# Layer 1's first product as seven block products, in a four-layer graph network on one Trainium2 core

## Chip, cores and metric

The kernel runs on one core of one Trainium2 chip. The metric is device time in microseconds (us) of one execution of the whole program: 2461.91 us is the median of 7 runs (2461.26 to 2463.57). All data are 32-bit floats, in the matrix products too. The engines are named as the profile names them: PE (TensorE, matrix products), PEld (its weight loads), DVE (VectorE), ACT (ScalarE), POOL (GpSimd), SP (SyncE, which issues most transfers).

## What is computed

128 graphs of 64 nodes with 256 features pass through four layers, each with a residual and a layer norm around it. Layer 0 is a gated graph network of five steps; layer 1, which the change touches, multiplies by a 256 x 1024 matrix, norms, and multiplies back; layer 2 is a hyperbolic aggregation; layer 3 an attention. Cut to what matters:

```python
# layer 0, five times (l = 0..4)
m = einsum('bnd,de->bne', h, weight[l])
agg = einsum('bij,bid->bjd', A, m)
h = gru_cell(agg, h, w_ih, w_hh, b_ih, b_hh)

# layer 1
neighbor_sum = einsum('bnm,bmd->bnd', adjacency, x)
agg = epsilon * x + neighbor_sum
h = einsum('bnd,dh->bnh', agg, W1) + b1          # 256 -> 1024, "the first product"
h = silu(h * rsqrt(mean(h*h, axis=-1) + 1e-6) * rms_weight)
out = einsum('bnh,hd->bnd', h, W2) + b2          # 1024 -> 256
```

The inputs hold `b1` = 0, `rms_weight` = 1 and `epsilon` = 0, but the kernel computes with whatever it is given.

## The kernel before, in words

**Tiling.** The graphs are taken in 16 groups of 8. Two graphs make one block of 128 rows, so a group is `NB` = 4 blocks, `R` = 512 rows. Most of a group's data is held with features on the 128 partitions: an array (128, `KD` = 2, 512) is 256 features by 512 rows; `HR` = 256 is half of the rows. `group(g)` writes all four layers of one group as a list of operations ("a stream"); the setup of weights is a stream ahead of them.

**Order.** Nothing is issued in program order. Each operation is put into a `Flow` with its engine, an assumed duration, what it reads and what it writes. `Flow.issue` then simulates the five engines over up to four streams at once (a `Plan`), in stretches of 25 us; for each stretch it extends every kept plan by three ranking rules and keeps the 8 plans with the smallest bound on the end. The order found becomes a fixed order for each engine. The assumed durations are written in `pe`, `turn`, `dve`, `act` and `pool`; the delay from one engine to the next is `HOPS`. At most three groups are in flight, because each group takes its buffers from one of `NF` = 3 sets (`unit(tag, s, ...)`; two operations that use the same tag and set share memory, the later waits for the earlier). PE's results go to 8 banks of 2 KB per partition (`bank`); a bank is free again after the last operation that uses it.

**Matrix products.** A product of a 128 x 128 weight tile with 256 or 512 columns is one `matmul` call. The profile holds two MATMUL records and two LDWEIGHTS records for each call, so four calls appear as "x8". In layer 0 the gates' 256 x 256 products over two halves of the rows are already made as seven block products (`gated`): `product(ps, w, v, ...)` adds four calls of 256 columns to a bank, DVE forms the differences (`minus`, L708) and adds the banks up (`plus`, L725). Three of its banks are read half-way and then added to: `p1` is copied by ACT (L755) before the second product goes onto it, and `pv` and `pw` are read by DVE (L725) before theirs. The second product has to wait for that read.

**Layer 1 before.** `aggm` (256 features x 512 rows) is multiplied by `w1s`, the whole of W1. For each of `KH` = 8 chunks of 128 hidden features: two calls of 512 columns into one bank `ps_hid` (L322), an ACT copy with the bias `b1c` added into `hid` (L827), an ACT square with the same bias (L830), and a DVE addition into `sqs` (L833). Four small calls then sum `sqs` over the features (`ps_ss`), POOL raises to -1/2, and the result is spread over the partitions (`ps_rms`, L843). For each chunk DVE multiplies `hid` by the RMS weight `rmsc` and by `ps_rms` (L848), ACT takes tanh of half of it (L851), and DVE makes silu times two of the two (L853). 32 calls with `w2s` give `ps_o` (L322).

**Setup that the change touches.** `w1s` and `w2s` come by one SP transfer each. `a_r`, `junk_d` and `a_sum` are fixed buffers used in setup alone; `a_r` is filled by a POOL transfer (`everywhere`).

Of the kernel before, what the change touches and what calls it, by code (L numbers as in the profile page):

```python
# [16 lines left out]
P = 128  # L17
# [25 lines left out]
class Op:  # L43
    __slots__ = ("eng", "us", "run", "stream", "n", "kb", "need", "then", "bufs", "opens", "id", "way")

    def __init__(self, eng, us, run, stream, n, kb):
        self.eng, self.us, self.run, self.stream, self.n, self.kb = eng, us, run, stream, n, kb
        self.need, self.then, self.bufs, self.opens, self.id, self.way = 0, [], (), None, 0, 0.0


class Plan:
# [25 lines left out]
    def advance(self, until, rank):  # L77
# [3 lines left out]
        while self.left and clock["PE"] < until:  # L81
# [29 lines left out]
            for b in o.bufs:  # L111
                n = self.uses.get(b, b.left) - 1
                self.uses[b] = n
                if not n:
                    banks.append(end + flow.hop(o.eng, "PE"))
                    banks.sort()
# [5 lines left out]
            for u in o.then:  # L122
                need[u.id] -= 1
                at[u.id] = max(at[u.id], end + flow.hop(o.eng, u.eng))
# [16 lines left out]
class Flow:  # L141
# [13 lines left out]
    HOPS = {"from PE": 0.25, "to PE": 0.3, "else": 0.1}  # L155
# [4 lines left out]
    WINDOW, STRETCH, WIDTH, LAG = 4, 25.0, 8, 40.0  # L160

# [9 lines left out]
    def op(self, eng, us, run, w=(), r=(), kb=0):  # L171
        o = Op(eng, us, run, len(self.streams) - 1, len(self.ops), kb)
# [31 lines left out]
    def hop(self, e, to):  # L204
        if e == to:
            return 0.0
        return self.HOPS["from PE" if e == "PE" else "to PE" if to == "PE" else "else"]

    def ways(self):
# [4 lines left out]
        for ops in self.streams:  # L214
            longest = 0.0
            for o in reversed(ops):
                path[o] = o.us + max((path[u] + self.hop(o.eng, u.eng) for u in o.then if u.stream == o.stream), default=0.0)
                o.way = longest = max(longest, path[o])
        self.work = sum(o.us for ops in self.streams for o in ops if o.eng == "PE")

    def issue(self):
# [3 lines left out]
        while any(p.left for p in plans):  # L225
            until += self.STRETCH
# [6 lines left out]
            plans = [found[k] for k in sorted(found)[:self.WIDTH]]  # L233
# [16 lines left out]
def kernel(  # L250
# [79 lines left out]
    def dve(n, run, w, r):  # L330
        flow.op("DVE", 0.16 + 0.00105 * n, run, w, r)

    def act(n, run, w, r):
        flow.op("ACT", 0.27 + 0.00077 * n, run, w, r)
# [73 lines left out]
    half_b = fixed([P, NV], "half_b")  # L408
# [59 lines left out]
    dve(300, halves, [half_b], [cols])  # L468

# [21 lines left out]
    def ih_out(i, k, ps):  # L491
        n = 512 if i == 0 else D
        act(n, lambda: nc.scalar.copy(wihT[k][:, i * 512:i * 512 + n], ps[:, :n]), [(wihT[k], i)], [ps])
# [4 lines left out]
    for l in range(L):  # L498
# [10 lines left out]
        for k in range(KD):  # L509
            for i, n in ((0, 2 * D), (1, D)):  # L510
# [5 lines left out]
                for dst, at in (((a11[l], 0), (a21, D)) if i == 0 else ((w_in[l], 0),)):  # L516
                    act(256, lambda ps=ps, k=k, dst=dst, at=at: nc.scalar.copy(dst[:, k, :], ps[:, at:at + D]),
# [8 lines left out]
    w1s = fixed([P, KD, H], "w1s")  # L526
    flow.op("SP", 0.6, lambda: nc.sync.dma_start(w1s.tile(), w1.rearrange("(k p) h -> p k h", p=P)), [w1s], kb=1024)
# [5 lines left out]
    def everywhere(v, n, name):  # L533
        t = fixed([P, n], name)
# [7 lines left out]
    a_r = everywhere(a_w, 2 * D, "a_r")  # L542
# [11 lines left out]
    junk_d = fixed([P, D], "junk_d")  # L554
# [4 lines left out]
    cs, a_sum = fixed([P, 1], "cs"), fixed([P, D], "a_sum")  # L559
# [14 lines left out]
    def group(g):  # L574
# [15 lines left out]
        def feats_of(dst, src, n):  # L590
# [7 lines left out]
            act(512, lambda: nc.scalar.copy(dst[:, :, half(n)], blocks_of(ps.tile())), [(dst, n)], [ps])  # L598
# [11 lines left out]
        def aggregate(dst, src, b0, n):  # L610
# [7 lines left out]
            act(512, lambda: nc.scalar.copy(dst[:, :, half(n)], blocks_of(ps.tile())), [(dst, n)], [ps])  # L618
# [11 lines left out]
        def layer_norm(y, tag, name, norm=None):  # L630
# [9 lines left out]
            pool(1.1, lambda: nc.gpsimd.tensor_tensor(rstd[:, :m, :], ve[:, :m, :], pow2[:, :m, :], OP.pow), [rstd], [ve])  # L640
# [7 lines left out]
            for b in range(NB):  # L648
                if b % 2:
                    act(300, lambda b=b: nc.scalar.activation(  # L650
                        o[:, b, :], y[:, b, :], AF.Identity, bias=off[:, b:b + 1], scale=rstd[:, 0, b:b + 1]),
                        [(o, b)], [(y, b), off, rstd])
                else:
                    dve(240, lambda b=b: nc.vector.tensor_scalar(
# [23 lines left out]
        def gated(l, h):  # L678
# [5 lines left out]
            def sides(n):  # L684

                if l:
                    ps = rows_of(h, n)
                    act(512, lambda: nc.scalar.copy(hr[:, 2 * n:2 * n + 2, :], blocks_of(ps.tile())),
# [4 lines left out]
                for c in range(KD):  # L693
                    act(300, lambda c=c: nc.scalar.activation(  # L694
# [32 lines left out]
            def tanh_half(o, src, i, r):  # L727
                for c in range(KD):
                    act(256, lambda c=c: nc.scalar.activation(  # L729
# [6 lines left out]
            def new_n(n, t):  # L736
# [4 lines left out]
                for c in range(KD):  # L741
                    act(256, lambda c=c: nc.scalar.activation(t[:, c, :], t[:, c, :], AF.Tanh, bias=bih(2 * KD + c)),
# [12 lines left out]
            act(420, lambda: nc.scalar.copy(uu.tile(), blocks_of(p1.tile())), [uu], [p1])  # L755
# [38 lines left out]
        for n in range(2):  # L794
            ps = rows_of(hT, n)
            for j in range(2):
                b = 2 * n + j
                blk = g * NB + b
                dve(256, lambda ps=ps, b=b, j=j, blk=blk: nc.vector.scalar_tensor_tensor(
# [15 lines left out]
        pool(2.35, lambda: nc.gpsimd.tensor_tensor(xb.tile(), x1.tile(), over(b2_r.tile(), NB), OP.add), [xb], [x1, b2_r])  # L815
        hid = []
        for i, tag in enumerate(("h", "h", "B", "A")):
            t = u(tag, f"hid{i}", (P, KD, R))
            hid += [(t, 0), (t, 1)]
        sqs = u("U", "sqs")  # L820
        for c in range(KH):
            ps = bank("ps_hid")
            for k in range(KD):
                pe(512, lambda ps=ps, k=k, c=c: matmul(
                    ps.tile(), w1s[:, k, c * P:(c + 1) * P], aggm[:, k, :], k, KD), [ps], [w1s, aggm])
            hc = hid[c]
            act(512, lambda ps=ps, hc=hc, c=c: nc.scalar.activation(  # L827
                hc[0][:, hc[1], :], ps.tile(), AF.Identity, bias=b1c(c)), [hc], [ps, cols])
            sq = u("ZR"[c % 2], f"sq{c}") if c else sqs
# [175 lines left out]
```

## Time and profile before

| | |
|---|---|
| median of 7 runs | 2461.91 us |
| the profiled execution: its own time | 2461.3 us |
| its span, first to last instruction | 2459.5 us |
| PE busy | 2417.6 us |
| PEld busy | 2042.0 us |
| DVE busy | 1707.4 us |
| ACT busy | 1233.8 us |
| POOL busy | 181.2 us |
| mean granted PE clock | 0.994 |
| data moved | 35.11 MB, mean 14 GB/s |

Busy time is the union of an engine's records, so overlapping records (PE's are pipelined) count once, and a record's mean duration is longer than the step from one record to the next. "Idle before" in a row is the time that the engine stood still just ahead of that row's instructions, and the name behind it is what ended the wait. A line number can be that of a helper: L322 is every plain `matmul`, L625 every call of `product`.

### The profile page before, as it was taken

Reading aid. Unit: us, or ns where it says so; the run is one execution under the profiler, and the core shown is the slowest. Engines: PE = TensorE matmul, PEld = TensorE weight load, DVE = VectorE, ACT = ScalarE, POOL = GpSimd, SP = SyncE. Lnnn points to the kernel's source line nnn. Section 1 sums busy time; section 2 is a strip of 40 time slices with the busy share of each in tenths; the row PEclk is TensorE's granted clock in tenths of the full one; section 3 lists DMA queues with packets and bytes.
Section 4 is the critical chain, followed back from the end, with each engine's and each line's share of the span. In section 5 each row is a group of like instructions: output and inputs, shape, how many; then the busy total and the mean of one; then the engine's idle time right before and its main releaser. Section 6 shows DMA issues by size and latency. Waiting matters only on the chain.

```text
span 2459.5 us, 31915 instructions
## 1 busy us (share of the span) xinstructions
PE 2417.6 (98%) x11922; PEld 2042.0 (83%) x11922; DVE 1707.4 (69%) x3741; ACT 1233.8 (50%) x2612; POOL 181.2 (7%) x144
## 2 busy tenths in 40 slices
PE   9999999999999999999999999999999999999995
PEld 7887887878788887888878788788888878878864
DVE  3656776767777767776776777677676767856776
ACT  3445455454545545454554544555554554454453
POOL 4000000000000000000000000000000000000011
PEclk9999999999999999999999999999999999999997
DMA  3000000000000000000000000000000000000000
GB/s 127 1 5 7 1 27 2 1 28 1 28 1 28 1 18 12 1 29 1 18 12 1 28 1 26 3 15 14 1 29 1 1 29 1 27 1 1 10 17 17
DMA packets 39145, 35.11 MB, mean 14 GB/s; under 512 B 9892, under 2 KB 38592, under 8 KB 38992
## 3 DMA queue, kind: packets, MB, share of 16 engines
q1 hardware_dynamic: 37264, 31.20, 3.9%
q8 instruction: 94, 1.54, 0.3%
q10 hardware_dynamic: 1328, 1.31, 0.2%
q0 software_dynamic: 400, 0.57, 0.1%
q14 instruction: 59, 0.48, 0.1%
HBM read 24.69 MB, written 8.39 MB: 13 GB/s over the span
## 4 chain that ended last, share of the span: by engine, by line
PE 73%; DVE 3%; ACT 1%; POOL 0%; issue 0%; POOLq 0%; ACTq 0%; DVEq 0%
PE p_v L625 9%; PE p_w L625 8%; PE p_r L625 8%; PE p_in L625 8%; PE p_hn L625 8%; PE ps_o L322 8%; PE ps_hid L322 8%; PE ps_agg L322 5%; PE p_u L625 4%; PE ps_hr L605 2%; PE ps_a L322 2%; PE ps_sup L322 1%; PE ps_att L322 1%; PE ps_T L595 1%; PE ps_ss L322 0%; DVE st L635 0%
## 5 line engine op out<-in xcount | busy, mean ns | idle before, releaser
L625 PE MATMUL p_hn<-hT,w_hn 128*128 128x256 f32 x1280 | 320.9, 380 | 0.1
L625 PE MATMUL p_in<-agg,w_in 128*128 128x256 f32 x1280 | 312.8, 379 | 0.0
L625 PEld LDWEIGHTS p_in<-agg,w_in 128*128 128x128 f32 x1280 | 240.9, 190 | 32.0 <-issue 0.5
L625 PEld LDWEIGHTS p_hn<-hT,w_hn 128*128 128x128 f32 x1280 | 229.0, 191 | 27.0 <-issue 2.6
L322 PE MATMUL ps_o<-w2s,hid 128*128 128x256 f32 x1024 | 229.8, 379 | 1.8 <-DVE hid L853 1.7
L322 PE MATMUL ps_hid<-aggm,w1s 128*128 128x512 f32 x512 | 224.1, 592 | 0.1
L322 PEld LDWEIGHTS ps_o<-w2s,hid 128*128 128x128 f32 x1024 | 193.7, 190 | 29.1 <-DVE hid L853 2.8
L640 POOL TENSOR_TENSOR rstd<-ve,pow 128x4 f32<-128x4 f32 (+1 forms) x64 | 82.0, 1281 | 1577.2 <-DVE ve L638 1568.9
L322 PEld LDWEIGHTS ps_hid<-aggm,w1s 128*128 128x128 f32 x512 | 96.5, 190 | 111.4 <-issue 108.5
L618 ACT COPY agg<-ps_agg 128x512 f32<-128x512 f32 x160 | 93.6, 585 | 149.2 <-PE ps_agg L322 123.1
L729 ACT ACTIVATE V<-V,half_b 128x256 f32<-128x256 f32 x160 | 73.0, 501 | 183.8 <-DVE V L725 183.7
L694 ACT ACTIVATE hnb<-p_hn,half_b 128x256 f32<-128x256 f32 x320 | 136.1, 472 | 55.6 <-PE p_hn L625 53.7
L625 PE MATMUL p_w<-tA,s 128*128 128x256 f32 x640 | 160.7, 379 | 0.0
L625 PE MATMUL p_v<-tB,s 128*128 128x256 f32 x640 | 159.4, 380 | 0.0
L625 PE MATMUL p_u<-tA,s 128*128 128x256 f32 x640 | 155.5, 380 | 1.5 <-DVE tA L708 1.4
L625 PE MATMUL p_w<-hT,s 128*128 128x256 f32 x640 | 156.6, 379 | 0.0
L625 PE MATMUL p_r<-hT,a 128*128 128x256 f32 x640 | 155.2, 379 | 0.2
L625 PE MATMUL p_v<-tB,na 128*128 128x256 f32 x640 | 154.7, 379 | 0.7 <-DVE V L725 0.7
L625 PE MATMUL p_r<-agg,a 128*128 128x256 f32 x640 | 154.0, 379 | 0.0
L833 DVE TENSOR_TENSOR sqs<-sqs,sq 128x512 f32<-128x512 f32 x112 | 77.3, 690 | 104.8 <-ACT sq L830 104.6
L322 PEld LDWEIGHTS ps_agg<-edge,hr 128*128 128x128 f32 x1024 | 137.2, 191 | 8.6 <-issue 1.4
L322 PE MATMUL ps_agg<-edge,hr 128*128 128x128 f32 x1024 | 139.1, 275 | 0.0
(205 smaller groups left out, 4430.9 us busy)
## 6 DMA issues: line engine op xcount, KB each, us to landing
x<-in_x_dram SPq DMA_DIRECT2D x16, 512.0 KB, 3.4
xr<-in_x_dram SPq DMA_DIRECT2D x16, 512.0 KB, 3.3
out_dram<-x_n SPq DMA_DIRECT2D x16, 512.0 KB, 2.9
edge<-in_adj_dram SPq DMA_DIRECT2D x32, 64.0 KB, 2.3
wm<-in_L_gnn_weight_dram SPq DMA_DIRECT2D x5, 256.0 KB, 5.0
w1s<-in_L_gnn_W_dram SPq DMA_DIRECT2D x1, 1024.0 KB, 6.2
w2s<-in_L_gnn_W_dram SPq DMA_DIRECT2D x1, 1024.0 KB, 10.1
aw_in_L_gnn_w_hh_dram<-in_L_gnn_w_hh_dram ACTq DMA_DIRECT2D x1, 512.0 KB, 5.3
```

The costliest lines, as they stand in the source:

```text
L322: return nc.tensor.matmul(o, lhsT, rhs, start=(k == 0), stop=(k == nk - 1))
L595: turn(lambda j=j, c=c: nc.tensor.transpose(ps[:, c * HR + j * P:c * HR + (j + 1) * P], src[:, 2 * n + j, c * P:(c + 1) * P], ident.tile() ...
L605: turn(lambda j=j, c=c: nc.tensor.transpose(ps[:, j * D + c * P:j * D + (c + 1) * P], src[:, c, (2 * n + j) * P:(2 * n + j + 1) * P], iden ...
L618: act(512, lambda: nc.scalar.copy(dst[:, :, half(n)], blocks_of(ps.tile())), [(dst, n)], [ps])
L625: pe(256, lambda c=c, k=k: nc.tensor.matmul(ps[:, c * HR:(c + 1) * HR], w[:, k, c * P:(c + 1) * P], v(k), start=first and c == k == 0, sto ...
L640: pool(1.1, lambda: nc.gpsimd.tensor_tensor(rstd[:, :m, :], ve[:, :m, :], pow2[:, :m, :], OP.pow), [rstd], [ve])
L694: act(300, lambda c=c: nc.scalar.activation(hnb[:, c, half(n)], p_hn[:, c * HR:(c + 1) * HR], AF.Identity, bias=half_b[:, 2 * KD + c:2 * K ...
L729: act(256, lambda c=c: nc.scalar.activation(o[:, c, :], src(c), AF.Tanh, bias=half_b[:, i * KD + c:i * KD + c + 1], scale=0.5), [(o, c)], ...
L833: dve(512, lambda sq=sq: nc.vector.tensor_add(sqs.tile(), sqs.tile(), sq.tile()), [sqs], [sqs, sq])
```

## The change

**The product.** `w1s` is replaced by `w1f`, seven 128 x 512 arrays made in setup from W1's four blocks `m11, m12, m21, m22` (features 0-127 and 128-255 by hidden units 0-511 and 512-1023): `m11`, `m12`, minus `m22`, and four sums. `aggm` is taken as four blocks too (its two feature halves by its two halves of the rows), DVE forms four differences `t1` to `t4` of them, and for each half `q` of the hidden units in a block, seven products are made, each of two calls of 256 columns. Three banks are read half-way and then added to (`p1`, `pv`, `pw`). ACT copies two results to `hid` (`onto`), DVE adds the rest up (`add`).

**Bias and RMS weight.** The bias is added in the square (as before) and in DVE's multiplication by `ps_rms` (where the RMS weight stood). The RMS weight goes into the scale of tanh (`half_r`, half the weight) and into `w2s`, whose eight 128 x 256 parts ACT scales once in setup.

**The search.** The assumed durations of ACT's, DVE's and some of POOL's operations are other numbers; the delay between engines is the sum of one number for the first engine and one for the second, less `early` of the operation; it also applies between two operations of one engine other than PE. In the last 350 us of PE's work the stretches are half as long and 24 plans are kept.

**Buffers.** `a_r`, `junk_d` and `a_sum` move into buffers of set 2 that groups use later.

```diff
-    HOPS = {"from PE": 0.25, "to PE": 0.3, "else": 0.1}
+    AFTER = {"PE": 0.2, "DVE": 0.12, "ACT": 0.13, "POOL": 0.04, "SP": 0.5}
+    BEFORE = {"PE": 0.1, "DVE": 0.0, "ACT": 0.0, "POOL": 0.05, "SP": 0.1}
+    ENDGAME = 350.0
...
-    def hop(self, e, to):
-        if e == to:
-            return 0.0
-        return self.HOPS["from PE" if e == "PE" else "to PE" if to == "PE" else "else"]
+    def hop(self, o, to):
+        return 0.0 if o.eng == to == "PE" else self.AFTER[o.eng] + self.BEFORE[to] - o.early
...
-            until += self.STRETCH
+            late = until > self.work - self.ENDGAME
+            until += self.STRETCH / 2 if late else self.STRETCH
...
-            plans = [found[k] for k in sorted(found)[:self.WIDTH]]
+            plans = [found[k] for k in sorted(found)[:self.WIDTH * (3 if late else 1)]]
...
     def dve(n, run, w, r):
-        flow.op("DVE", 0.16 + 0.00105 * n, run, w, r)
+        flow.op("DVE", 0.075 + 0.00105 * n, run, w, r)
-    def act(n, run, w, r):
-        flow.op("ACT", 0.27 + 0.00077 * n, run, w, r)
+    def act(us, run, w, r, early=0.0):
+        flow.op("ACT", us, run, w, r, early=early)
...
+    dve(4, lambda: nc.vector.tensor_scalar(half_r.tile(), cols[:, 2 * NV + KH:], 0.5, None, OP.mult), [half_r], [cols])
...
-    w1s = fixed([P, KD, H], "w1s")
-    flow.op("SP", 0.6, lambda: nc.sync.dma_start(w1s.tile(), w1.rearrange("(k p) h -> p k h", p=P)), [w1s], kb=1024)
+    HH = H // 2
+    w1k = w1.rearrange("(k p) h -> p k h", p=P)
+    m11, m12, mn22, ms1, ms2, ms3, ms4 = range(7)
+    w1f = fixed([P, 7, HH], "w1f")
+    for at, src, kb in ((slice(m11, m12 + 1), w1k[:, :, :HH], 512), (slice(ms4, ms4 + 1), w1k[:, 0:1, HH:], 256),
+                        (slice(mn22, mn22 + 1), w1k[:, 1:2, HH:], 256)):
+        flow.op("SP", 0.6, lambda at=at, src=src: nc.sync.dma_start(w1f[:, at, :], src),
+                [(w1f, i) for i in range(at.start, at.stop)], kb=kb)
+    for o, x0, x1, op in ((ms1, ms4, mn22, OP.add), (ms3, m11, ms4, OP.subtract), (ms2, ms1, m11, OP.subtract), (ms4, m12, ms2, OP.subtract)):
+        dve(512, lambda o=o, x0=x0, x1=x1, op=op: nc.vector.tensor_tensor(
+            w1f[:, o, :], w1f[:, x0, :], w1f[:, x1, :], op), [(w1f, o)], [(w1f, x0), (w1f, x1)])
+    dve(512, lambda: nc.vector.tensor_scalar(w1f[:, mn22, :], w1f[:, mn22, :], -1.0, None, OP.mult), [(w1f, mn22)], [(w1f, mn22)])
...
-    a_r = everywhere(a_w, 2 * D, "a_r")
+    a_r = everywhere(a_w, 2 * D, "a_r", unit("V", S, "a_r", (P, 2 * D)))
...
+    for k in range(KH):
+        act(0.4, lambda k=k: nc.scalar.activation(w2s[:, k, :], w2s[:, k, :], AF.Identity, scale=rmsc(k)), [(w2s, k)], [(w2s, k), cols])
...
+        def prod(ps, w, v, q, first, last):
+            for c in range(2):
+                pe(256, lambda c=c: nc.tensor.matmul(
+                    ps[:, c * HR:(c + 1) * HR], w1f[:, w, (2 * q + c) * P:(2 * q + c + 1) * P], v[0](),
+                    start=first and c == 0, stop=last and c == 1, skip_group_check=True), [ps], [(w1f, w), v[1]])
+        def add(o, ps, x):
+            dve(512, lambda: nc.vector.tensor_add(o[0], blocks_of(ps.tile()), x[0]), o[1], [ps, *x[1]])
+        def onto(ps, o):
+            act(0.49, lambda: nc.scalar.copy(o[0], blocks_of(ps.tile())), o[1], [ps])
+        diff(s_t1, b12, b11)
+        diff(s_t2, b22, s_t1)
+        diff(s_t3, b22, b12)
+        diff(s_t4, s_t2, b21)
         sqs = u("U", "sqs")
-        for c in range(KH):
-            ps = bank("ps_hid")
-            for k in range(KD):
-                pe(512, lambda ps=ps, k=k, c=c: matmul(
-                    ps.tile(), w1s[:, k, c * P:(c + 1) * P], aggm[:, k, :], k, KD), [ps], [w1s, aggm])
-            hc = hid[c]
-            act(512, lambda ps=ps, hc=hc, c=c: nc.scalar.activation(
-                hc[0][:, hc[1], :], ps.tile(), AF.Identity, bias=b1c(c)), [hc], [ps, cols])
-            sq = u("ZR"[c % 2], f"sq{c}") if c else sqs
-            act(512, lambda ps=ps, sq=sq, c=c: nc.scalar.activation(sq.tile(), ps.tile(), AF.Square, bias=b1c(c)),
-                [sq], [ps, cols])
-            if c:
-                dve(512, lambda sq=sq: nc.vector.tensor_add(sqs.tile(), sqs.tile(), sq.tile()), [sqs], [sqs, sq])
+        for q in range(2):
+            (c11, c12), (c21, c22) = ([block(i, n) for n in range(2)] for i in (q, 2 + q))
+            p1, pu, pv, pw = (bank(f"p_{n}h") for n in "1uvw")
+            prod(p1, m11, b11, q, True, False)
+            onto(p1, c12)
+            prod(p1, m12, b21, q, False, True)
+            onto(p1, c11)
+            prod(pu, ms2, s_t2, q, True, True)
+            add(c12, pu, c12)
+            prod(pv, ms3, s_t3, q, True, False)
+            add(c22, pv, c12)
+            prod(pw, ms1, s_t1, q, True, False)
+            prod(pv, mn22, s_t4, q, False, True)
+            add(c22, pw, c22)
+            add(c21, pv, c12)
+            prod(pw, ms4, b22, q, False, True)
+            add(c12, pw, c12)
+            for c in (4 + 2 * q, 5 + 2 * q, 2 * q, 2 * q + 1):
+                v, parts = chunk(c)
+                sq = u("Z", f"sq{c}") if q or c != 4 else sqs
+                act(0.535, lambda v=v, sq=sq, c=c: nc.scalar.activation(sq.tile(), v, AF.Square, bias=b1c(c)), [sq], [*parts, cols])
+                if sq is not sqs:
+                    dve(512, lambda sq=sq: nc.vector.tensor_add(sqs.tile(), sqs.tile(), sq.tile()), [sqs], [sqs, sq])
...
-            dve(512, lambda hc=hc, c=c: nc.vector.scalar_tensor_tensor(
-                hc[0][:, hc[1], :], hc[0][:, hc[1], :], rmsc(c), ps_r.tile(), OP.mult, OP.mult), [hc], [hc, ps_r, cols])
+            dve(512, lambda v=v, c=c: nc.vector.scalar_tensor_tensor(
+                v, v, b1c(c), ps_r.tile(), OP.add, OP.mult), parts, [*parts, ps_r, cols])
             th = u("VZR"[c % 3], f"th{c}")
-            act(512, lambda hc=hc, th=th: nc.scalar.activation(th.tile(), hc[0][:, hc[1], :], AF.Tanh, scale=0.5),
-                [th], [hc])
+            act(0.535, lambda v=v, th=th, c=c: nc.scalar.activation(th.tile(), v, AF.Tanh, scale=half_r[:, c:c + 1]),
+                [th], [*parts, half_r])
```

## The prediction

> **What bounds the kernel now.** I read the page's busy times first, then the same by stages, then the chain of waits, then the rows of the operations that come and go.
>
> ```profile
> PE 2417.6 (98%) x11922; PEld 2042.0 (83%) x11922; DVE 1707.4 (69%) x3741; ACT 1233.8 (50%) x2612; POOL 181.2 (7%) x144
> 60.00:2340.00 2280.00, 2275.95 (x11339) 1938.81 (x11338) 1603.90 (x3422) 1155.68 (x2448) 137.67 (x99) 1.00 0.04 11
> 2340.00:2353.50 13.50, 13.50 (x34) 6.08 (x33) 11.54 (x38) 9.73 (x16) 1.33 (x1) 1.00 0.11 39
> 2353.50:2365.00 11.50, 7.23 (x40) 6.43 (x39) 8.46 (x20) 4.98 (x9) 4.33 (x3) 0.85 0.01 2
> 2365.00:2378.50 13.50, 13.50 (x32) 5.89 (x31) 9.43 (x16) 11.47 (x19) 0.00 (x0) 1.00 0.00 1
> 2378.50:2385.00 6.50, 6.50 (x37) 5.82 (x36) 1.40 (x3) 1.27 (x2) 1.02 (x1) 1.00 0.00 0
> ```
>
> The first line is the whole span; the others are stretches with their length, then the busy time of PE, PEld, DVE, ACT and POOL. Between 60 and 2340 us PE stands still for 2280.00 - 2275.95 = 4.05 us: there the end is set by the amount of PE work. Of the 42 us that PE is idle in all (2459.5 - 2417.6), some 35 lie after 2353.5, where only the last two groups are left. So two questions decide: how much PE work goes, and what happens in those last 106 us.
>
> **The product.** The chain of waits (start, length, what) gives steady prices:
>
> ```profile
> 793.38 13.73 PE ps_hid L322 x32
> 774.70 1.73 PE p_w L625 x8
> ```
>
> Before: 8 chunks x 2 calls of 512 columns, 32 records, 13.73 us per group. After: 2 halves x 7 products x 2 calls of 256 columns = 28 calls. Four such calls (x8) take 1.73, so 28 take 7 x 1.73 = 12.11. Saved: 1.62 per group, x 16 groups = **25.9 us**.
>
> This rests on 256 columns costing half of 512. Per record it is 1.73 / 8 = 0.2163 against 13.73 / 32 = 0.4291, a ratio of 0.504. Each half-length record still has its own weight load, and that is the limit to watch:
>
> ```profile
> L322 PEld LDWEIGHTS ps_hid<-aggm,w1s 128*128 128x128 f32 x512 | 96.5, 190 | 111.4 <-issue 108.5
> L625 PE MATMUL p_v<-tB,na 128*128 128x256 f32 x640 | 154.7, 379 | 0.7 <-DVE V L725 0.7
> L755 ACT COPY U<-p_r 128x512 f32<-128x512 f32 x48 | 27.9, 581 | 34.0 <-PE p_r L625 34.0
> L827 ACT ACTIVATE hid<-ps_hid,cols 128x512 f32<-128x512 f32 x128 | 87.9, 687 | 54.6 <-PE ps_hid L322 54.1
> L830 ACT ACTIVATE sq<-ps_hid,cols 128x512 f32<-128x512 f32 x112 | 76.3, 681 | 0.0
> ```
>
> A load takes 190 ns and hides under a step of 216 ns, as it already does in layer 0. Break-even would be 13.73 / 28 = 0.490 per call against 0.433.
>
> A page speaks against short products: the Trainium skill, "TensorE: Matmul & The Clock Gate", section Back-to-back issue gap, gives load-and-product pairs 81 ns at 128 columns and 131 at 512. A straight line between them puts 256 columns at 97.7 ns, so 28 calls would take 28 x 97.7 / (16 x 131) = 1.31 times the old block; as an estimate from that page, 4.2 us more per group and some 2528 us in all. The chain's 0.504 says otherwise for these 32-bit products, and the measurement decides.
>
> **Other engines, per group.** DVE gains 10 additions of 128x512 out of PSUM (L725 rows, 0.69 us: 6.9) and 4 differences of 128x256, a form not shown: half of a 512 difference is 0.35, the 256-wide operation L963 takes 0.48; I take 0.42 between them, 1.7. Together 8.6. ACT loses 8 copies with bias (0.687: 5.5) and gains 4 plain copies (0.585, as L618 and L755: 2.3); squares stay. So ACT has 3.2 less. DVE is at 1603.90 / 2280 = 70% in the long stretch, 105.5 us per 150 us that a group takes; afterwards (105.5 + 8.6) / 148.4 = 77%. Still no bound.
>
> **New waits in the long stretch.** In each half a product is put onto `p1` after ACT's copy and onto `pv` and `pw` after DVE's addition: 3 x 2 x 16 = 96 waits. Uncovered, one costs PE's end to the reader's start, 0.2 (ps_rms to DVE at 2385.0), plus the reader and its way back: 0.64 for ACT (x3T copied at 2440.86, ps_a at 2441.50), and for DVE 0.69 plus the 0.15 that tan took to release ps_sup (2402.18 to 2402.33). That is 0.84 and 1.04, mean 0.97, and PE's queue is in order, so all that is behind it waits too. Cover is other groups' products. Layer 0 has the same three waits per step, 240 in all, and the idle time before `p_r<-hT,a`, `p_v<-tB,na` and `p_w<-hT,s` is 0.2 + 0.7 + 0.0 = 0.9 us: 0.4% of their price. At that share 96 x 0.97 costs 0.4 us. Each half needs four banks instead of one at a time; layer 0 holds six to eight. Bounds: 0 and 12 us (three times the present 4.05 us more, as the new durations leave the plan less slack: DVE of 512 to PE is now planned at 0.83 us where the row needs 0.84, before at 1.0). I take 0.4, by the rows of the same pattern.
>
> **The last 106 us.** Both last groups make the product here, the very last at 2365. From 2340 to 2385 DVE is busy 11.54 + 8.46 + 9.43 + 1.40 = 30.8 of 45.0 us. With 2 x 8.6 it needs 48.0, and the stretch is 2 x 1.62 shorter: 41.8. DVE becomes late by 6.2, and its late work is what the remaining `ps_o` products wait for. Bounds: 0 (the order shifts work into DVE's idle time, ACT having 6.4 less) and 17.2 (none fits). I take 6.2.
>
> Against it stands the search, which keeps more plans here and prices ACT's two table loads around Ln. PE's waits in this stretch that a better order could shorten:
>
> ```profile
> PE ps_T L595 <- DVE x_n L654: 12.7, 2, 10.1
> PE ps_sup L322 <- DVE tan L900: 5.1, 1, 5.1
> PE ps_ss L322 <- DVE sqs L833: 1.9, 1, 1.9
> PE ps_o L322 <- DVE hid L853: 1.7, 2, 1.0
> PE ps_agg L322 <- DVE x_n L654: 1.4, 1, 1.4
> ```
>
> The 10.1 is mostly the last group's own chain. The others make 12.7 - 10.1 + 5.1 + 1.9 + 1.7 + 1.4 = 12.7. Bounds: a gain of 12.7, and a loss of the same size, since another order is another draw. I take a gain of 4, a third.
>
> **Setup at nothing.** SP issues two more transfers (0.47 each, the w1s row at 12.45) for the same 1024 KB; behind them in its queue stand w2s and group 2's adjacency, which goes out at 13.43 and is first turned at 23.72, so 0.9 us later is covered. DVE gets five 512-wide operations and a tiny one (3.6 us), ACT eight 256-wide ones (0.375 to 0.475: up to 3.8). PE is busy 75 of the 75 us from 25 to 100, DVE 11.05 and ACT 11.92 of the 35 from 25 to 60, and the first `ps_hid` starts at 216.7. `a_r` on POOL's queue must now wait until `wm1` was turned (about 25); POOL's next work starts at 33.29. Uncovered, all this is 8.3 us.
>
> **Sum**, against the profiled execution's own 2461.3 us (span 2459.5 and 1.8 around it): 2461.3 - 25.9 + 0.4 + 6.2 - 4 = **2438.0**. That execution lies 0.6 below the median of 2461.91, so a median might read 2438.6; I stay at 2438.
>
> **Rivals.**
> A. The end pays in full: DVE's 17.2 exposed, no gain from the search. 2461.3 - 25.9 + 0.4 + 17.2 = 2453. For it: DVE busy 11.54 of 13.5 where group 14 makes its product. Against: 1.40 of 6.5 just after.
> B. The additions hide and the search shortens the end by 10 of its 12.7: 2461.3 - 25.9 + 0.4 - 10 = 2426. For it: ACT is relieved, and DVE stands idle a quarter of the last 100 us. Against: most of those waits are one group's own chain.
> C. Slower: PE stands at the half-read banks `p1`, `pv`, `pw`. It decides once 25.9 / 0.97 = 27 of the 96 waits are bare; at half of them, 46.6 us, the time is 2461.3 - 25.9 + 46.6 = 2482. For it: a product here is two calls (0.87 us), in layer 0 four (1.73), so less of the group's own work covers each. Against: 0.9 us over 240 such waits.
> D. The product doesn't get cheaper: calls cost near the break-even of 0.490, as bare weight loads would make them. About 2461. Against: the 216 ns step under the same load in 7040 records of layer 0.
>
> **Chances.** Forecast 65%, A 14%, B 11%, C 6%, D 4%. The forecast's own range is 2431 to 2447. Faster by over 0.2% (4.9 us, about what a measurement here can tell from none): the forecast, A and B, 90%. Within it: most of D, 3%. Slower: C and the rest of D, 7%. The range of 8 in 10 reaches over A and B, 2424 to 2454, leaving out C, D and the outer ends of A and B.
>
> **What would show it.** The group of 512-column `ps_hid` records is gone; 896 records of 256 columns with `w1f` stand at about 379 ns in steps of 0.216; PE busy falls to some 2392, ACT to 1180, DVE rises to 1845. PE's idle time between 60 us and the start of the last groups stays near 4 us; much more says C, with releasers ACT `hid` or DVE `hid`. PE's idle time at the end near 37 us says forecast, near 52 A, near 25 B. Steps above 0.24 would say D. The forecast is wrong if PE busy falls by less than 20 us, or if its idle time grows by over 15.

## The result, and the profile after

The changed kernel takes **2469.26 us**, median of 14 runs (2467.12 to 2470.91), against 2462.01 us for the kernel before in 34 runs beside them: a ratio of 1.0029 (95% interval 1.0022 to 1.0036). It is slower by 7 us. (Medians here leave out one execution each of the kernels of experiments 2 and 8, which fell into a slower state.) The forecast was 2438, with a range of 2424 to 2454: wrong in size and in sign.

The page's busy times after the change:

```profile
PE 2418.4 (98%) x12306; PEld 2100.6 (85%) x12306; DVE 1774.4 (72%) x3971; ACT 1202.7 (49%) x2554; POOL 175.0 (7%) x144
```

Two stretches of it (length, then busy PE, PEld, DVE, ACT, POOL):

```profile
60.00:2340.00 2280.00, 2265.30 (x11600) 1976.82 (x11598) 1644.72 (x3609) 1124.09 (x2392) 147.63 (x115) 1.00 0.04 12
2340.00:2385.00 45.00, 39.98 (x203) 33.54 (x202) 38.63 (x79) 20.62 (x38) 7.76 (x5) 1.00 0.04 12
```

PE's busy time did not fall at all (2417.6 before), though the work did. Idle time between 60 and 2340 us is 14.7 us, 4.05 before: 10.7 more, a third of what is missing. The product itself is as cheap as forecast. Groups of the new product (busy, mean ns of one record, idle before):

```profile
L855 PE MATMUL p_vh<-t,w1f 128*128 128x256 f32 x256 | 68.1, 383 | 3.4 <-DVE t L851 3.4
L855 PE MATMUL p_1h<-aggm,w1f 128*128 128x256 f32 x256 | 67.5, 385 | 3.6 <-ACT hid L863 3.6
L855 PE MATMUL p_wh<-aggm,w1f 128*128 128x256 f32 x128 | 33.1, 380 | 0.0
```

They add up to 896 records with the two that are left out, each 380 to 385 ns long. Where they run unbroken the step is 0.216 us.

**A busy PE hides stalls.** A record lasts 383 ns but the next one starts 216 ns later, so the union of records (PE's busy time) stays closed until a start is late by more than 383 - 216 = 167 ns, and of any longer stall it shows only the rest. I therefore measured, from the same traces, the time between the starts of successive MATMUL records less the steady step of that shape (0.2163 us for 256 columns, 0.4291 for 512, 0.1095 for 128). This "lost time" sees a late start of any size; a PE that runs slower, as it does for some us in the end, is counted in it too. In microseconds; "work" is the sum of the steady steps, "small" are stalls of 0.03 to 0.4 us and "long" those above, with their number; "middle" runs from 60 us to 120 us before the end, "end" is the rest, and "new" is the part of the middle lost just ahead of a new product:

```
                     median   span   | work    first 60  middle  small       long       end  | new
before               2462.0   2459.5 | 2402.5   3.2       7.2     4.2  (36)   4.2  (4)  44.2 |  -
after                2469.3   2467.5 | 2376.6   4.5      41.4    27.6 (256)  14.3 (16)  42.7 | 11.4
```

Work, first 60, middle and end, with the 2.5 us before the first product, make the span. The change of 8.0 us in span is, but for rounding, -25.9 (work) + 1.3 + 34.2 (middle) - 1.5 (end). The work fell by just what was forecast, the middle gave it all back, and 30 of its 41.4 us are not at the new product: 62 stalls at layer 0's `p_u` cost 11.3 us, 55 at `ps_o` 4.7, 41 at `p_v` 4.4. Not every one of the 256 small stalls is a wait of its own: 56 of them, 5.8 us, are 0.10 us between the first and the second record of a product that itself started late.

One small stall in the timeline of the changed kernel (start, length, engine, line, operation; in brackets the engine's idle time and what ended it):

```profile
606.04 0.59 ACT L639 COPY agg<-ps_agg 128x512 f32<-128x512 f32 x1
606.66 0.69 DVE L729 TENSOR_TENSOR tB<-hT,ps_agg 128x512 f32<-128x512 f32 x1 [0.65 <-ACT agg L639]
607.27 0.68 DVE L765 TENSOR_TENSOR hT<-hT,R 128x512 f32<-128x512 f32 x1
607.40 1.13 PE L646 MATMUL p_v<-tB,s 128*128 128x256 f32 x4
607.87 0.69 DVE L729 TENSOR_TENSOR tA<-hT,tA 128x512 f32<-128x512 f32 x1
608.61 1.99 PE L646 MATMUL p_u<-tA,s 128*128 128x256 f32 x8
```

`p_v`'s four records from 607.40 are due to be followed at 607.40 + 4 x 0.2163 = 608.27; `p_u` starts at 608.61 because `tA` ends at 608.56: 0.34 us lost, 0.10 of it inside `p_v`, which had started late itself, and 0.24 ahead of `p_u`. Yet `p_v`'s records end at 608.53, so PE counts as idle for only 0.08. The chain shows such places without any table: a link `p_u` x8 that had to wait is given 1.99, one that follows without a break 1.73 (the third line, of the same kernel, and the links of before).

```profile
608.61 1.99 PE p_u L646 x8
726.28 1.99 PE p_u L646 x8
1463.07 1.73 PE p_u L646 x8
```

The other thing in this timeline is the first pair. DVE stood idle 0.65 us until ACT had finished its copy of the same bank `ps_agg`, although the two only read it. The groups of that read in the kernel before (mean ns of one, then idle ahead of it and what ended that):

```profile
L708 DVE TENSOR_TENSOR tA<-ps_agg,agg 128x512 f32<-128x512 f32 x80 | 55.0, 688 | 55.8 <-PE ps_agg L322 49.0 <-ACT agg L618 5.1
L708 DVE TENSOR_TENSOR tB<-hT,ps_agg 128x512 f32<-128x512 f32 x80 | 54.3, 678 | 0.0
```

And in the changed kernel:

```profile
L729 DVE TENSOR_TENSOR tA<-ps_agg,agg 128x512 f32<-128x512 f32 x80 | 55.0, 687 | 31.8 <-ACT agg L639 22.0 <-PE ps_agg L326 9.4
L729 DVE TENSOR_TENSOR tB<-hT,ps_agg 128x512 f32<-128x512 f32 x80 | 54.3, 678 | 9.8 <-ACT agg L639 9.8
```

DVE waits for ACT here 22.0 + 9.8 us; before, 5.1. (Before, it was more often ACT that waited: its copy `agg` stood 24.7 us for `tA`, in 40 waits, and 6.0 us after.) `tB`'s 9.8 are 15 waits of 0.65 us, a copy's length; of `tA`'s 22.0, 15.2 are three waits of over 4 us, in which DVE stood until ACT came to the copy at all. Of DVE's 160 reads only 5 overlap a copy, and none of them the copy of its own bank, when both are followed bank by bank in the order in which the kernel issues them. The wait ends at a semaphore of ACT's copy: the order is in the program. The planner does not know it: it counts what an operation reads and writes, and two readers are free of each other in it.

And one long stall:

```profile
1826.05 2.36 POOL L836 TENSOR_TENSOR xb<-x_n,b_r 128x1024 f32<-128x1024 f32 x1 [1.52 <-ACT x_n L671]
1826.36 2.60 DVE L759 SCALAR_TENSOR_TENSOR R<-R,hnb 128x512 f32<-128x512 f32 x1 [0.99 <-ACT R L750]
1827.65 1.03 PE L855 MATMUL p_1h<-aggm,w1f 128*128 128x256 f32 x4
1829.06 0.69 DVE L761 TENSOR_TENSOR R<-p_in,R 128x512 f32<-128x512 f32 x1
1829.67 0.75 DVE L851 TENSOR_TENSOR t<-aggm 128x256 f32<-128x256 f32 x2
1830.14 0.70 PE L855 MATMUL p_wh<-t,w1f 128*128 128x256 f32 x2 [1.45 <-DVE t L851]
```

A DVE operation that takes 0.69 us elsewhere takes 2.60 while POOL's addition `xb` runs beside it, and PE, which takes its products in the plan's fixed order, stands for 1.45 us at the `t` behind it. There are 10 such collisions after the change and 11 before. In the 6 us behind them PE lost 12.1 us of the middle after, 10.9 of it in long stalls (of their 14.3), and 4.7 before, 4.2 of it in long stalls (all of them): the collisions are old, what covered them has gone.

### The profile page after: what moved, and what is told of

Its sections match the earlier page's. It is cut to its first block, busy times and chain, and to the rows that moved or that the text cites. A ratio compares the mean times of both kernels' runs of the same rounds, so it can differ in the third digit from the quotient of the medians.

```text
span 2467.5 us, 32883 instructions
## 1 busy us (share of the span) xinstructions
PE 2418.4 (98%) x12306; PEld 2100.6 (85%) x12306; DVE 1774.4 (72%) x3971; ACT 1202.7 (49%) x2554; POOL 175.0 (7%) x144
## 4 chain that ended last, share of the span: by engine, by line
PE 86%; DVE 9%; ACT 3%; issue 1%; POOL 0%; DMA 0%; ACTq 0%; POOLq 0%; DVEq 0%
PE p_r L646 11%; PE p_w L646 10%; PE p_in L646 10%; PE p_v L646 10%; PE p_hn L646 9%; PE ps_o L326 9%; PE ps_agg L326 5%; PE p_u L646 5%; PE ps_a L326 2%; PE ps_hr L626 2%; PE p_vh L855 2%; PE p_wh L855 2%; PE p_1h L855 2%; PE p_uh L855 1%; PE ps_att L326 1%; PE ps_sup L326 1%
## 5 line engine op out<-in xcount | busy, mean ns | idle before, releaser
L326 PE MATMUL ps_o<-w2s,hid 128*128 128x256 f32 x1024 | 236.3, 385 | 4.0 <-DVE hid L913 4.0
L326 PEld LDWEIGHTS ps_o<-w2s,hid 128*128 128x128 f32 x1024 | 190.1, 191 | 41.1 <-DVE hid L913 12.1
L646 PE MATMUL p_u<-tA,s 128*128 128x256 f32 x640 | 160.7, 383 | 4.2 <-DVE tA L729 2.5
L759 DVE SCALAR_TENSOR_TENSOR R<-R,hnb 128x512 f32<-128x512 f32 x80 | 60.0, 750 | 119.1 <-ACT R L750 118.8
L646 PEld LDWEIGHTS p_u<-tA,s 128*128 128x128 f32 x640 | 117.2, 190 | 29.4 <-issue 8.2
L750 ACT ACTIVATE R<-p_r,half_b 128x256 f32<-128x256 f32 x160 | 68.5, 470 | 149.9 <-PE p_r L646 149.9
L646 PEld LDWEIGHTS p_v<-tB,s 128*128 128x128 f32 x640 | 118.9, 190 | 22.0 <-DVE tB L729 5.3
```

Source lines behind the costliest of these rows:

```text
L326: return nc.tensor.matmul(o, lhsT, rhs, start=(k == 0), stop=(k == nk - 1))
L646: pe(256, lambda c=c, k=k: nc.tensor.matmul(ps[:, c * HR:(c + 1) * HR], w[:, k, c * P:(c + 1) * P], v(k), start=first and c == k == 0, sto ...
L750: act(0.4, lambda c=c: nc.scalar.activation(o[:, c, :], src(c), AF.Tanh, bias=half_b[:, i * KD + c:i * KD + c + 1], scale=0.5), [(o, c)], ...
L759: dve(512, lambda: nc.vector.scalar_tensor_tensor(t.tile(), t.tile(), 1.0, hnb[:, :, half(n)], OP.add, OP.mult), [t], [t, (hnb, (n, 0)), ( ...
```

## Experiments

The question at first: does the new product make PE stand (my rival C), or do the planner's new durations and delays? All ratios are to the kernel before, with 95% intervals; the lost time is given as in the table above. Diffs are against the changed kernel.

**1. The product with the old durations and delays.**

```diff
-    AFTER = {"PE": 0.2, "DVE": 0.12, ...}; BEFORE = {"PE": 0.1, ...}; ENDGAME = 350.0
+    HOPS = {"from PE": 0.25, "to PE": 0.3, "else": 0.1}; ENDGAME = -1e9
-        flow.op("DVE", 0.075 + 0.00105 * n, run, w, r)
+        flow.op("DVE", 0.16 + 0.00105 * n, run, w, r)
-            act(0.49, ...)
+            act(0.664, ...)
...
```

> The seven block products with the assumed durations, the delays between engines and the search of the kernel before (the search's part undone). Theory S (the new durations leave the plan no slack, and PE stands at hand-overs everywhere): PE's lost time between 60 and 2340 us falls from 41 us to about 10, and the time is about 2462 - 26 + 4 = 2440 us. Rival P (the product itself: its half-read banks and 8.6 us more of DVE per group): the loss stays near 40 us and the time at 2465 to 2472 us.

2455.84 us, ratio 0.997 (0.9958 to 0.9981), between the two forecasts. Middle 18.3 us (small 5.5, long 14.2), end 52.1. Alone the product gains, but 7 us and not 26: 11.1 go in the middle, nearly all in long stalls, and 7.9 at the end. At the new product itself only 3.8 are lost.

**2. The old product with the new durations, delays and search.** The old loop over `ps_hid` with `w1s` is put back, bias and RMS weights too.

> The old first product, bias and RMS weight with the new durations, delays and search (the search's part alone). Theory S: PE loses some 25 to 35 us at hand-overs of the gates, about 2485 us. Rival P: the new search costs nothing, 2450 to 2463 us.

> The old product with the new durations, delays and search once more, for its trace. Theory S: PE's lost time between 60 and 2340 us is made of stalls below 0.4 us, some 20 us or more of them (7 us lost in all before), and few long ones. Rival P: the small stalls stay near the 4 us of before and something else makes the 2478 us.

2476.29 us, ratio 1.0061 (1.0045 to 1.0078), and 2476.16 in one more execution, whose trace is read here. The time lies between the two forecasts; the lost time is near theory S's, with more long stalls than it had. Middle 34.2 (small 21.7 in 193 stalls, long 12.8), end 30.6. So the new numbers alone (the wider search acts in the last 350 us only) cost 27 us in the middle, with not one new product in the kernel, and bring 13.6 at the end. Together with experiment 1 this decides between product and plan: most of the loss is the plan's. The parts don't add (11.1 + 27.0 = 38.1; both together give 34.2).

**3. More slack ahead of PE.**

```diff
-    BEFORE = {"PE": 0.1, "DVE": 0.0, "ACT": 0.0, "POOL": 0.05, "SP": 0.1}
+    BEFORE = {"PE": 0.25, "DVE": 0.0, "ACT": 0.0, "POOL": 0.05, "SP": 0.1}
```

> The changed kernel with one number changed: the planned delay onto PE 0.25 instead of 0.1 us. Theory S: the hand-overs get their slack back, loss in the long stretch about 15 us, 2440 to 2448 us. Rival P: no change, 2465 to 2472 us.

2446.52 us, ratio 0.9935 (0.992 to 0.995). One number, 23 us: small stalls fall from 27.6 (256) to 11.3 (126), long ones from 14.3 to 8.5. The result of a 512-wide DVE operation was planned to reach PE 0.83 us after the operation's start, now 0.98. In the changed kernel's stalls it takes 0.74 (41 of 71, as `tA` above: 607.87 to 608.61) or 0.84 us (the other 30). So this hand-over by itself was not planned short on average. In the timeline it is the start of DVE's operations that came late, because `tB` had to wait for ACT; slack ahead of PE covers such lateness from further back as well.

**4. The old delays with the new durations.**

> The changed kernel with the old delays between engines (0.25 from PE, 0.3 to PE, 0.1 else, none within an engine), but the new durations and the new search. Theory S, delays being the larger part of it (0.08 more onto PE from DVE, durations the other 0.09): about halfway, 2450 to 2460 us. Rival P: 2465 to 2472 us.

2547.13 us, ratio 1.0344 (1.0328 to 1.0359): both forecasts missed, by 75 us and more. Middle 108.8, of it 67.9 in 72 long stalls. The old delays are nothing inside an engine, and with the shorter durations a chain of DVE operations of 4 elements is planned at 0.079 a link (0.20 with the new delay), where the trace of before shows links at 2397.52, 2397.71, 2397.92 and 2398.12, 0.20 apart. Its largest waits of PE (total, times, longest):

```profile
PE ps_T L617 <- DVE x_n L676: 16.3, 6, 9.1
PE p_u L647 <- DVE tA L730: 12.6, 27, 2.1
PE p_v L647 <- DVE V L747: 9.3, 10, 1.8
```

The layer norm's chain of such operations ends in `x_n`, the first row. The new durations leave out what the delay within an engine adds, so the two belong together. That this explains the other rows too is my reading; no run restores this delay alone.

**5. The old durations with the new delays.**

> The changed kernel with the new delays and search but the old, longer durations of DVE and ACT (512 columns on DVE 0.70 instead of 0.61 us). Theory S (slack anywhere on the way to PE will do): small stalls fall from 27 to below 10 us, 2445 to 2455 us. Rival (only slack on PE's own side helps): 2462 to 2470 us.

2452.7 us, ratio 0.9964 (0.9951 to 0.9977), small stalls 8.7: slack by another door, with the same effect on the middle (18.1), though the end (49.9) is nearly as long as in experiment 1. What counts is the slack in the sum of duration and delay, and in every link of the way: experiment 4 plans the last one, a 512-wide DVE operation to PE, at 0.91 us, and still loses.

**6. The POOL addition on DVE.**

```diff
-        pool(2.4, lambda: nc.gpsimd.tensor_tensor(xb.tile(), ...
+        dve(1080, lambda: nc.vector.tensor_tensor(xb.tile(), ...
```

> The changed kernel with the addition that makes xb moved from POOL to DVE (1.2 us of DVE per group, POOL has no long operation left). Theory L (DVE operations that overlap POOL's xb take 2.2 to 2.7 instead of 0.69 us and cause PE's long stalls, 12 us of them within 6 us after): long DVE operations vanish, PE's stalls above 0.4 us fall from 14 to about 4 us, the small ones stay near 27 us, time 2456 to 2462 us. Rival (the long stalls come from the half-read banks and DVE's load, which now grows by 20 us in all): 2469 to 2480 us.

2464.61 us, ratio 1.001 (1.0001 to 1.0019); I had expected 3 to 9 us less. Long stalls fall nearly as expected, from 14.3 to 5.6, though DVE gains 16 operations of 1.22 us. Small stalls rise from 27.6 to 29.7, and the end grows by 3.0.

**7. Slack and ACT's prices; slack and POOL.** The square and the tanh take 719 and 720 ns as records and follow each other in steps of 0.63 us, planned at 0.535. One kernel takes slack 0.25 and 0.63 for both, the next moves `xb` to DVE as well.

> The changed kernel with the planned delay onto PE 0.25 us and the square and tanh planned at 0.63 instead of 0.535 us, the step that the trace shows for them with a bias or a scale from memory. Theory S in full (every price set too low makes stalls): small stalls fall below 10 us, 2438 to 2445 us. Rival (only the delay onto PE mattered): 2446 to 2448 us, as with the delay alone.

> The kernel with slack (0.25 us onto PE, square and tanh at 0.63) and xb on DVE instead of POOL. Theory L (POOL's xb holds DVE up and that makes PE's long stalls): stalls above 0.4 us fall from 10 to about 3 us, 2438 to 2442 us. Rival (DVE's 20 us more cost as much as they save): 2445 to 2450 us.

The prices change nothing: 2446.17 us, ratio 0.9935 (0.992 to 0.995), the same as experiment 3. With `xb` on DVE: 2436.61, ratio 0.9898 (0.9884 to 0.9913), long stalls 9.9 to 2.6, new 8.7 to 0.6. With slack in the plan, moving the addition brings 9.6 us; without it, 4.7.

**8. Still more slack, 0.4.**

> The kernel with slack, the planned delay onto PE 0.4 instead of 0.25 us. Theory S: the small stalls, 10 us at 0.25 and 27 at 0.1, fall to about 5 us; if the plan can still cover so long a delay, 2440 to 2444 us. Rival (what is left is not of the hand-overs, and a longer delay costs plan time): 2446 to 2455 us.

2443.55 us, ratio 0.9929 (0.991 to 0.9949). The long stalls fell (9.9 to 4.5), the small ones did not (10.0 to 11.1). So about 10 us of small stalls do not go with more slack of this kind. This is what sent me to the idle rows of DVE above.

**9. ACT and DVE on one bank.** `t1` and `t3` read ACT's copy in SBUF instead of the bank that ACT is copying.

```diff
-            a2 = lambda: blocks_of(p_a2.tile())
-            minus(t1, a2, of(a, 0), [p_a2, (a, 0)])
+            a2 = of(a, 1)
+            minus(t1, a2, of(a, 0), [(a, 1), (a, 0)])
...
-            minus(t3, of(h, 1), a2, [(h, 1), p_a2])
+            minus(t3, of(h, 1), a2, [(h, 1), (a, 1)])
```

> The changed kernel, new times as they are; only the gates' first and third difference read the aggregate from its copy in SBUF instead of from the bank that ACT copies at the same time. In the trace ACT's copy and DVE's differences out of one bank almost never overlap (5 pairs of 160), which the plan does not know. Theory B (this hidden order makes a good part of the small stalls: those before p_u and before p_v from tB, 15 of 27 us): these fall below 5 us, 2455 to 2461 us. Rival (the hand-overs are short of slack whatever the source): 2466 to 2474 us.

2459.03 us, ratio 0.9989 (0.998 to 0.9999): 10 us below the changed kernel, by an edit that removes no work and adds a wait to the plan. Stalls before `p_u` and `p_v` fall from 15.5 to 3.2 us, small ones from 27.6 to 19.0. Those at the new product rise at the same time, from 11.4 to 18.3 us, so the 10 us are what is left over. DVE's groups in this kernel:

```profile
L729 DVE TENSOR_TENSOR tA<-agg 128x512 f32<-128x512 f32 x80 | 54.7, 683 | 5.8 <-ACT agg L639 5.4
L729 DVE TENSOR_TENSOR tB<-hT,agg 128x512 f32<-128x512 f32 x80 | 54.6, 683 | 0.0
```

The wait was in the changed kernel all along (22.0 + 9.8 us); now the planner knows of it and puts other work there (5.4 + 0.0).

**10. The old product in the last two groups** (slack 0.25, ACT's prices): 16 calls of 512 columns from the same `w1f`.

> The kernel with slack, where the last two groups make the first product by 16 calls of 512 columns again (the four chunks of the second half from the stored sums, with one more difference on DVE). Theory T (in the end, where DVE sets the pace, the block products cost some 12 us: PE's lost time after 2340 us and the time after the last product make 41 us with them and 29 with the old product): the end falls to about 30 us, for 3.2 us more of PE, 2436 to 2440 us. Rival (the end is one group's own chain, whatever the product): 2447 to 2450 us.

2440.5 us, ratio 0.9913 (0.9898 to 0.9928), against 2446.17 without. Work grows by 3.2, the end falls from 41.3 to 33.0. From 2340 to 2400 us (busy PE, PEld, DVE, ACT, POOL), without the edit:

```profile
2340.00:2400.00 60.00, 52.67 (x234) 44.02 (x233) 48.45 (x99) 28.07 (x44) 7.41 (x5) 0.91 0.00 1
```

With it:

```profile
2340.00:2400.00 60.00, 55.26 (x225) 38.78 (x223) 44.77 (x116) 33.23 (x60) 10.13 (x7) 1.00 0.00 1
```

ACT takes up what DVE had: with two groups left there is little other work to cover DVE's sums. A part of the gain is PE's clock, the third number from the end: 0.91 without the edit, 1.00 with it. Without it PE ran at a granted clock of 0.5 for 3.4 us three times, from 2345.4, 2362.5 and 2372.7, beside pauses of 2.72, 1.81 and 1.39 us; 18 records of 256 columns there have a step of up to 0.43 us, not 0.216, which makes 3.7 us. With the edit there is none between 2340 and 2400.

**11. The parts together.** First the old product with what the new one got (slack 0.25; then also `xb` on DVE), so that the product is judged at equal care:

> The old product with the new durations and search, and the planned delay onto PE 0.25 us. Theory S: the small stalls go, 2455 to 2463 us, so that the product's worth at equal slack is 10 to 17 us against 2446.5 us. Rival (the new search hurts the old product for another reason): 2470 to 2479 us.

> The old product in all groups with the new search, 0.25 us onto PE, and xb on DVE. If POOL's xb hurts only where DVE is as loaded as the block products make it: no gain, 2456 to 2460 us, and the product's worth at equal care is 20 us and more. If it hurts any plan: 2450 to 2454 us, worth 14 to 17 us.

2458.48 (0.9976 to 0.9995 of before) and 2455.74 us (0.9960 to 0.9982). Against 2446.17 and 2436.61 with the new product it is worth 12.3 and 19.1 us, out of 25.9 of work. Moving `xb` to DVE gains 2.7 us with the old product and 9.6 with the new one. Then all edits in one (slack, ACT's prices, `xb` on DVE, the old product in the last two groups), with slack 0.25 or 0.4, and both also with `t1` and `t3` from SBUF:

> Slack (0.25 us onto PE, square and tanh at 0.63), xb on DVE, and the old product in the last two groups. If the three losses are separate: 2436.6 - 6 (what the last two groups gave) = 2429 to 2433 us. If the end's gain and xb's gain are the same waits: 2436 to 2438 us.

> The same three with 0.4 us onto PE. Going from 0.25 to 0.4 gave 2 us before: 2427 to 2432 us; if xb on DVE has taken those waits already, no difference to the one with 0.25.

> The best kernel so far (0.4 us onto PE, square and tanh at 0.63, xb on DVE, old product in the last two groups, 2425.5 us) with the same two differences from SBUF. Theory B: 2419 to 2424 us. Rival: slack has covered these waits already, 2425 to 2430 us.

> The same with 0.25 instead of 0.4 us onto PE (2430.4 us without the differences from SBUF). If the longer delay was needed only because of the hidden order, this gains more than the one with 0.4: 2420 to 2425 us. If it covers something else too: 2427 to 2431 us.

```
                                  median   ratio (interval)           | work    first 60  middle  small       long       end
all three, 0.25                   2430.37  0.9869 (0.9852 to 0.9885)  | 2379.8   4.8      10.6     9.6  (97)   2.1  (4)  30.9
all three, 0.4                    2425.49  0.9849 (0.9835 to 0.9864)  | 2379.8   5.0       8.2     8.1  (76)   1.3  (2)  28.7
same, 0.25, SBUF                  2425.68  0.9853 (0.9837 to 0.9870)  | 2379.8   5.5       7.8     7.1  (79)   2.0  (3)  27.6
same, 0.4, SBUF                   2423.33  0.9842 (0.9827 to 0.9856)  | 2379.8   5.5       4.1     3.8  (44)   1.6  (3)  29.9
```

The page of the last shows its busy times. It is the fastest of all, 39 us below the kernel before and 46 below the changed one. Reading `agg` from SBUF brings 4.7 us at slack 0.25 and 2.2 at 0.4, where the extra slack seems to cover part of that wait already. Of the four forecasts the first and the third hit their first range; the second and the fourth missed theirs by 1.5 and 0.7 us. The middle of the last one loses less (4.1) than before the change (7.2), with the new product in it:

```profile
PE 2392.7 (99%) x12258; PEld 2103.0 (87%) x12258; DVE 1758.3 (73%) x3961; ACT 1199.1 (50%) x2562; POOL 144.5 (6%) x128
```

PE busy 2392.7 is near what I had forecast for the changed kernel (2392). That is in part luck: the work here is 3.2 us more than the changed kernel's, and PE's busy time counts small stalls as work.

## Why the prediction was wrong

**PE's work, -25.9: right.** The sum of steady steps fell from 2402.5 to 2376.6. Rival D, calls dearer than half, is out; and the 2528 us worked out from the Trainium skill's figures do not describe these 32-bit products.

**"I take 0.4, by the rows of the same pattern": this step failed.** The term for new waits in the long stretch was 0.4, with a bound of 12; the middle lost 34.2 us more, most of it at products that the change did not touch. Three faults are in it.

*The instrument.* I read "0.9 us over 240 such waits" as proof that layer 0 covers them. But those rows show PE idle, and a stall of under about 0.17 us shows no idle at all. By starts, the middle of before lost 7.2 us and not 4.05, and after it 41.4 and not 14.7.

*The extent.* I did see that the new numbers plan 0.83 us where the row needs 0.84, and then bounded its effect by three times the idle time, for the 96 new waits. The missing slack acts at every hand-over to PE in the kernel: experiment 2, without one new wait, loses 27 us, and 0.15 us more slack gives 23 back. The 0.84 was also a single reading, at a PE that had stood for 5.1 us; in the changed kernel the same hand-over takes 0.74 or 0.84. So the price of the last link was not what failed; experiment 4 plans it at 0.91 and loses 108.8 us in the middle. In a plan without slack, lateness from further back runs on to PE, where a late hand-over holds up all that is behind it and an early one brings nothing. That last sentence is my reading; the runs show the two amounts.

*What the plan does not know.* The order of ACT and DVE on `ps_agg` and POOL's hold on DVE are in no duration of the plan. Both stood in the trace of before, in the 5.1 us (and ACT's 24.7) and in the 11 stretched DVE operations, and looked harmless, because they cost PE little there. Experiments 6 to 9 put 10 us on the first and 5 to 10 on the second.

**The end, +6.2 and -4: each sign right, the sizes and so the sum not.** Measured, the product makes the end longer by 12.1 (30.6 to 42.7 with the new search; 7.9 with the old numbers), and numbers and search together shorten it by 13.6 (44.2 to 30.6). Net -1.5, forecast +2.2. I took a third of the shortenable waits; it was just over all of the 12.7.

**Setup at nothing: nearly.** The first 60 us lost 1.3 more. (The transfer at 12.45 takes 0.37 us to issue, and not the 0.47 that I read; that belongs to the next one. The term is nothing either way.)

**Busy times.** ACT 1202.7, forecast 1180: square and tanh take 719 and 720 ns where the rows that they replaced took 681 and 629. To plan them at their true step changes nothing (experiment 7). DVE rose by 67 and not by 138: its records summed one by one rose by 130 (1857 to 1987), but they overlap by 63 us more. A record lasts 0.69 us, but operations that follow each other start 0.60 apart, as `hT` and `tA` above (607.27, 607.87), so a sum over rows overstates.

**The rivals.** C had the sign, and named releasers that do appear, ACT `hid` and DVE `t`. But its place is 11.4 of the 34.2 us, and 0.6 us with slack and without POOL's collision (experiment 7). What I never listed was that the planner's numbers could make all the rest of the kernel worse: I let the search enter at the end alone, with a loss of at most 12.7, while the kernel before and the one after differ in the order of everything.

**Still open.** Why the product alone brings 10 us of long stalls at the old numbers (experiment 1) was not taken apart: 5.8 of its 14.2 us lie behind its 8 collisions with POOL's addition, the rest elsewhere, and moving that addition was tried with the new numbers only. One link is planned short and no run corrects it: a DVE operation that needs the result of the 512-wide one just before it starts 0.79 us after that one's start (median of 103 in the changed kernel), planned 0.73. How much of the end's 13.6 us is the wider search and how much the new numbers was not tried. Each kernel is one order that a search found, and no run changes the order alone: of gains of 2 to 5 us, as those of reading `agg` from SBUF in experiment 11, a part may be the draw. What two reads of one bank at once would do, no run shows, since the program never lets it happen.

## What to carry to other kernels

In a kernel bound by one engine that works in a fixed order, measure lost time from start to start against the steady step before believing that nothing is lost: a busy share of 98% hid 27 us of stalls here. In a fixed order made from assumed durations, give every hand-over to the bound engine some slack beyond the measured time (0.15 us was worth 23 us here), and write down each conflict that is no data dependency: two readers of one bank, two engines of which one stops the other. Judge a saving of work and a change of the plan apart, each against the same slack: the product here is worth 12 to 19 us, and the numbers that came with it cost 27 in the long stretch.

## What the runs showed of the hardware

**Two readers of one PSUM bank take turns, by a semaphore.** Of DVE's 160 reads of `ps_agg` in the changed kernel none overlapped ACT's copy of the same bank, and DVE waited 31.8 us in all for such copies, each wait ended by the copy's semaphore. The Trainium skill, "PSUM — Partial Sum Buffer", section PSUM bank collisions raise a hardware error, says that two engines must not touch the same bank in the same partitions at once, reading included, and that the compiler's scheduler adds a dependency between any two such instructions. The order seen agrees; to read the copy in SBUF instead made this kernel 10 us faster in all.

**POOL stops DVE for a whole instruction.** Beside a 2.36 us addition on POOL, a DVE operation on two SBUF inputs took 2.60 us, not 0.69, and ended 0.55 us after POOL's. The same skill, "SBUF — State Buffer", section SBUF: two separate sides, says that such a pair holds one shared port by turns, each for its whole length. The row agrees, and moving the addition to DVE, where it takes 1.22 us, was worth 4.7 to 9.6 us with the new product and 2.7 with the old one, although DVE was much the busier engine.

**A weight load under a short product costs nothing here, as long as PE does not wait.** 896 records of the new product kept the step of 0.216 us where they run unbroken, with their 190 ns loads beside them. A product that starts late loses 0.10 us more at its second record: the four records of `p_v` at 607.40 take 1.13 us, four unbroken ones (`p_1h` at 1827.65) 1.03.
